# Causal attention in a two-layer kernel: the order of the key tiles within a head group, and the place of the one step without a dense part

## The chip, the core and the metric

The kernel is one program on one core of a Trainium2 chip. The metric is the device time of one launch in microseconds. Three runs of the kernel before took 1786.90, 1788.79 and 1789.57 us, so its median is 1788.79 us. One more execution was profiled; its own time and its span are in the table below.

## The reference, cut to what matters

Two layers work on x (2 batches of 1024 positions by 512 features). The first layer is a small recurrent block beside a gated feed-forward block; the change doesn't touch it. The second layer is causal attention beside a gated, 2:4-sparse feed-forward block. The change is in the attention:

```
qkv = x @ W_qkv.T + b_qkv ; q, k, v = split(qkv)         # 16 heads of 32 features
scores = einsum('bqhe,bkhe->bhqk', q, k) / sqrt(32)
scores = where(tril, scores, -inf)                        # a key counts for later queries only
out = einsum('bhqk,bkhe->bqhe', softmax(scores), v)
out = out.reshape(b, l, d) @ W_out.T + b_out
```

A softmax row is a sum over key tiles, so the tiles may be taken in any order.

## The kernel before, in words

Everything is in 32-bit floats. The attention stage runs from about 658 us to about 1198 us of the span. Ahead of it are the first layer, behind it the second feed-forward block. Within the stage the work is cut into eight **units** (batch bb, head group hg): four heads of one batch each.

**Two passes for each unit.** The first, `maxima` (L1179), computes scores for a query tile of 128 (qt 0 to 7) against a key chunk c of up to 512, and takes row maxima: TensorE writes two pairs of banks (L1188, tile m), VectorE adds the causal mask where the chunk holds the diagonal (L1195) and reduces (L1196). There are 12 of these a unit, of widths 128, 256, 384, 512, then (512, 128), (512, 256), (512, 384), (512, 512). The second pass has 12 **steps** a unit. A step is (j, kt): query half j (512 queries) against the key tile kt (128 keys). For j = 0 there are key tiles 0 to 3, for j = 1 key tiles 0 to 7. On the diagonal (kt >= 4j) only the queries from the tile on count, so the tile has 512, 384, 256 or 128 columns for kt - 4j = 0, 1, 2, 3; s in the code is the first column. Below, p is the place of a step in its unit, 0 to 11: p 0 to 3 are the first half, p 4 to 11 the second.

**One turn of the loop (L1492) for step n:**
1. `weights(n)` (L1238): TensorE writes the negated maxima (L1247) and adds the scores (L1253, tile s) into two bank pairs of two heads each. ScalarE takes the exponential of each pair into SBUF (L1264): into a tile `acc` for kt 0, else into one of five buffers `pt`. On the diagonal GpSimd cuts 128 columns to the causal triangle (L1273, affine select).
2. At fixed steps, parts of `shift_part` (L1216 on ScalarE, L1218 on GpSimd), which prepares the maxima of the next unit.
3. `gather(n-1)` (L1286): TensorE multiplies the weights of the step before with the values (L1297, tile o, one bank for a half), and the weights are added into `acc` (L1284) by GpSimd. The tile kt 6 of the second half goes to VectorE instead (`add_later`, L1301), after this turn's maxima. After the last key tile ScalarE copies o out (L1308).
4. At p 3 and p 7, transposes px of the shifted maxima (L1227) and `total` (L1312): TensorE sums `acc` (L1317, tile w), which gives the softmax denominators; four reciprocals on VectorE (L1329) and a product on GpSimd (L1333) follow over the next turns.
5. `do_first(n+13)`: the maxima, 13 places ahead. In p 0 to p 11 their widths are 256, 384, 512, 512, 128, 512, 256, 512, 384, 512, 512 and 128.
6. One **dense part** (L1047, 16 narrow matmuls): a seventh of a q/k projection of a later unit, half of a value tile, or half of a tile of the output projection. The first part of a projection also issues four weight sums on GpSimd (L1110 to L1112, L1153). `quiet` (L1484) names the turns without a dense part, p 6 of units 0 to 5; a part that is due is still forced by `late` (L1475).

**What sets the order.** `in_program_order` (L48) makes each engine execute the attention in the order in which the code issues it. The score pairs s, the maxima pairs m, px and w take turns in three wide PSUM tiles (`ps_wide`, L70), so each of them waits until the one three places before it has been read. `idle_vector` (L1234) tells the last 13 steps, which run beside no maxima: there VectorE takes over the masks and the sums. The values of key tile x are given due times (L1418 to L1427) such that they are there when o needs them.

Of the kernel before, what the change touches and what calls it, by code (L numbers as in the profile page):

```python
# [28 lines left out]
HG = NH * HD // P  # L29
# [6 lines left out]
def two_layers(ctx: ExitStack, tc: tile.TileContext, t: dict, out: bass.AP):  # L36
# [33 lines left out]
    def ps_wide(name):  # L70
        nonlocal wides
        wides += 1
        return ps_pair(name, wides % 3)

    def ps_bank(name, which):

        return ps.tile([P, 512], F32, tag=f"bank{which}", name=name)
# [278 lines left out]
    with tc.tile_pool(name="a", bufs=1) as a:  # L356
# [431 lines left out]
        for n in range(NU - 1):  # L788
            u = 2 * n + 2
# [89 lines left out]
        tt, next_tt, second = None, None, None  # L879
# [72 lines left out]
    with tc.tile_pool(name="b", bufs=1, reuse_waits="tile") as b:  # L952
# [74 lines left out]
        units = [(bb, hg) for bb in range(B) for hg in range(HG)]  # L1027
# [24 lines left out]
        def piece(name, lhs, rhs, done):  # L1052

            got = []

            def part(n):
                if n == 0:
                    got.append(next_bank(name))
                for k in (2 * n, 2 * n + 1):
                    dense(got[0], lhs(k), rhs(k), k == 0, k == KC - 1)  # L1060
                if n:
                    done(got[0])

            return [(part, 0), (part, 1)]
# [92 lines left out]
        def values(bb, n, j):  # L1157


            def done(pv):  # L1160
                if (bb, n, j) not in vals:
                    vals[bb, n, j] = b.tile(
                        [P, D], F32, tag="v", name=f"v_{bb}_{n}_{j}", bufs=12
                    )
                v = vals[bb, n, j]
                if alone is None:
                    nc.vector.tensor_add(v, pv, bv)
                else:
                    nc.scalar.copy(v, pv)
                    nc.gpsimd.tensor_add(v, v, bv)  # L1170

            return piece(
                f"pv_{bb}_{n}_{j}", lambda k: xt1[2 * bb + n][:, k, j * P : (j + 1) * P],
                lambda k: wv[:, k, :], done,
            )
# [55 lines left out]
            negs[u, half] = b.tile([P, TT], BF16, tag="neg", name=f"neg_{u}_{half}", bufs=4)  # L1231
            nc.vector.tensor_copy(negs[u, half], px[:, :NJ].rearrange("p t c -> p (t c)"))

        def idle_vector(u, j, kt):  # L1234

            return per * u + 4 * j + kt + ahead >= len(second)

        def weights(u, j, kt):  # L1238

            q, k, neg = qk[u, 0], qk[u, 1], negs[u, j]  # L1240
            name = f"{u}_{j}_{kt}"
            s = max(0, kt - 4 * j) * P
            cols = slice(j * 512 + s, (j + 1) * 512)
            pair = [ps_wide(f"s_{name}_{p}") for p in range(2)]
            for h in range(4):
                rows = slice(h * HD, h * HD + 3)
                nc.tensor.matmul(  # L1247
                    pair[h // 2][:, h % 2, s:], onesb[rows, :], neg[rows, s:],
                    start=True, stop=False,
                )  # L1250
            for h in range(4):
                rows = slice(h * HD, (h + 1) * HD)
                nc.tensor.matmul(  # L1253
                    pair[h // 2][:, h % 2, s:], k[rows, kt * P : (kt + 1) * P], q[rows, cols],
                    start=False, stop=True,
                )
            got = []
            for p in range(2):

                if kt == 0:  # L1260
                    pt = b.tile([P, 2, 512], F32, tag=f"acc{p}", name=f"acc_{name}_{p}", bufs=2)
                else:
                    pt = b.tile([P, 2, 512], F32, tag="pt", name=f"pt_{name}_{p}", bufs=5)
                nc.scalar.activation(  # L1264
                    pt[:, :, s:], pair[p][:, :, s:], AF.Exp, scale=1.0 / math.sqrt(HD)
                )
                d = pt[:, :, s : s + P]
                if kt >= 4 * j and idle_vector(u, j, kt - 1):
                    nc.vector.tensor_tensor(
                        d, d, allowed.unsqueeze(1).to_broadcast([P, 2, P]), ALU.min  # L1270
                    )
                elif kt >= 4 * j:
                    nc.gpsimd.affine_select(  # L1273
                        out=d, in_=d, compare_op=ALU.is_ge, fill=0.0,
                        base=0, pattern=[[0, 2], [1, P]], channel_multiplier=-1,
                    )
                got.append(pt)
            return u, j, kt, s, got
# [3 lines left out]
        def add_weights(eng, u, j, s, pts):  # L1282
            for acc, pt in zip(sums_of[u, j], pts):
                eng.tensor_add(acc[:, :, s:], acc[:, :, s:], pt[:, :, s:])  # L1284

        def gather(u, j, kt, s, pts):  # L1286

            bb, hg = units[u]
            if kt == 0:
                held[u, j] = ps_bank(f"o_{u}_{j}", 0)  # L1290
                sums_of[u, j] = pts
            po = held[u, j]
            last = kt == 4 * j + 3
            v = vals[bb, kt // NJ, kt % NJ][:, hg * P : (hg + 1) * P]
            for h in range(4):
                rows = slice(h * HD, (h + 1) * HD)
                nc.tensor.matmul(  # L1297
                    po[rows, s:], v[:, rows], pts[h // 2][:, h % 2, s:],
                    start=(kt == 0), stop=last, tile_position=(0, h * HD),
                )  # L1300
            if (j, kt) == (1, 6) and not idle_vector(u, j, kt):  # L1301

                add_later.append((nc.vector, u, j, s, pts))
            elif kt:
                add_weights(nc.vector if idle_vector(u, j, kt) else nc.gpsimd, u, j, s, pts)
            if last:
                att[u, j] = b.tile([P, 512], F32, tag="att", name=f"att_{u}_{j}", bufs=12)
                nc.scalar.copy(att[u, j], po)  # L1308
# [31 lines left out]
        def project_out(m):  # L1340
# [11 lines left out]
            (u, qt, c) for u in range(len(units)) for qt in range(QT) for c in range(qt // 4 + 1)  # L1352
        ]
        second = [
            (u, j, kt) for u in range(len(units)) for j in range(2) for kt in range(4 * j + 4)
        ]
        per, ahead = len(second) // len(units), 13

# [3 lines left out]
        rest, fixed, middle, after = [], {}, {}, {}  # L1362

        def put(n, *what):
            fixed.setdefault(n, []).append(what)
# [48 lines left out]
        rest = [(lo, hi, project(u)) for lo, hi, u in rest]  # L1414
# [1 line left out]
            put(per * 2 + n, next_sums)  # L1416
        put(per * 4 + 4, own_place)
        for x in range(4):  # L1418
            rest.append((-ahead, x, values(0, 0, x)))
            rest.append((-ahead, 7 + x, values(0, 1, x)))  # L1420
            for j in range(2):
                put(2 * x + j - 12, last_stats, 2 + x // 2, 2 * (x % 2) + j)
                put(2 * x - 9, last_row, 2 + x // 2, 2 * (x % 2) + j)
            put(2 * x - 10, last_norm, 2 + x // 2, x % 2)
            rest.append((per, per * 4 + x, values(1, 0, x)))

            rest.append((per * 3 + 5 + x, per * 4 + 2 + x, values(1, 1, x)))  # L1427
        put(per * 4 + 5, load_out)
# [52 lines left out]
            )  # L1481


        quiet = {per * u + 6 for u in range(6)}  # L1484
        behind = None
        start = mark()
        for _ in input_sums(0):
# [4 lines left out]
        for n in range(-ahead, len(second)):  # L1492
            if n == 0:
                alone = None
            now = weights(*second[n]) if n >= 0 else None
            for f, *args in middle.pop(n, ()):
                f(*args)
            if behind is not None:
                gather(*behind)
            behind = now  # L1500
            for f, *args in after.pop(n, ()):
                f(*args)
            if n < 0:
                one_part(n)
            if n + ahead < len(first):
                do_first(n + ahead)
            while add_later:
                add_weights(*add_later.pop())
            if (n >= 0 or n % 2) and n not in quiet:
                one_part(n)  # L1510
            while late(n) and one_part(n):
                pass
            what_is_fixed(n)
        in_program_order(start)
        gather(*behind)
        alone = 0
        narrow = False
# [14 lines left out]
    with tc.tile_pool(name="c", bufs=1, reuse_waits="tile") as c_:  # L1532
        units = [(pb, g, half) for pb in (1, 0) for g in range(G) for half in range(2)]
# [130 lines left out]
        for n in range(groups - 1):  # L1664

            end = n == groups - 2
            u = 2 * n + 2
# [49 lines left out]
        tt, next_tt, second = first_tt, None, None  # L1717
# [5 lines left out]
        for n, (pb, g, half) in enumerate(units):  # L1723
            i0 = 2 * pb
            x, y = xt1[i0], xt1[i0 + 1]
# [107 lines left out]
```

## Time and profile before

| | |
|---|---|
| median of three runs | 1788.79 us |
| the profiled execution: time | 1786.11 us |
| the profiled execution: span of its instructions | 1784.4 us |
| TensorE busy | 1753.4 us, 98% |
| VectorE, ScalarE, GpSimd busy | 1155.0, 481.0, 840.8 us |
| units 0 to 6 of the second pass, from the first L1247 matmul of each to the next one's | 58.0, 59.2, 59.6, 58.9, 59.2, 59.2, 58.6 us |
| unit 7 (no maxima), from 1136.5 us | 33.4 us to its last step's start |

Sum over the five middle units: 296.0 us. In the profile, PE is TensorE's matmuls, PEld its weight loads, DVE is VectorE, ACT is ScalarE, POOL is GpSimd and SP the queue of most DMAs. A row of the timeline gives the start, the duration, the engine, the source line, the operation, "out<-in" by tile names, and in brackets how long the engine sat idle before and what it waited for. Where rows are merged (x8), the duration is the union. Matmuls are pipelined, so the time that a group of them really costs is read from its start to the next group's start.

### The profile page before, as it was taken

What the parts mean: (1) busy time and instruction counts of PE and PEld (TensorE: products, weight loads), DVE (VectorE), ACT (ScalarE), POOL (GpSimd) and SP (SyncE); (2) the same over time, 40 slices, a digit from 0 to 9 for tenths busy, and PEclk for the clock granted to TensorE, in tenths of its full rate; (3) what the DMA queues carried; (4) which work ended last, traced back from release to release, by engine and by line L of the source; (5) the groups of instructions that cost most, each with busy time, mean ns of one, the idle gap of its engine ahead of it and who ended that gap; (6) DMA issues with size and microseconds to landing.
All of it is one profiled execution on the core that took longest, in us unless ns stands there. A gap on an engine that the chain in (4) does not pass through costs nothing.

```text
span 1784.4 us, 21717 instructions
## 1 busy us (share of the span) xinstructions
PE 1753.4 (98%) x8734; PEld 882.1 (49%) x8734; DVE 1155.0 (65%) x1516; ACT 481.0 (27%) x687; POOL 840.8 (47%) x736
## 2 busy tenths in 40 slices
PE   9999999999999999999999999999999999999999
PEld 5456566555555573322232222234565555555555
DVE  4875544556544367577677766842877778668676
ACT  3322222122221112433443443512221211211220
POOL 5145554355552243577868866613243344243400
PEclk9999999999999999999999999999999999999999
DMA  6120111011100000000000000011011102201101
GB/s 237 48 83 24 48 36 36 30 42 36 36 24 30 19 30 25 1 13 13 1 25 25 13 13 1 25 47 47 24 59 36 48 24 83 83 24 47 47 1 47
DMA packets 29619, 68.28 MB, mean 38 GB/s; under 512 B 3408, under 2 KB 11856, under 8 KB 27984
## 3 DMA queue, kind: packets, MB, share of 16 engines
q1 hardware_dynamic: 28800, 66.61, 10.8%
q8 instruction: 69, 1.13, 0.3%
q10 hardware_dynamic: 720, 0.30, 0.1%
q14 instruction: 30, 0.25, 0.0%
HBM read 62.70 MB, written 4.19 MB: 37 GB/s over the span
## 4 chain that ended last, share of the span: by engine, by line
PE 86%; POOL 7%; DVE 3%; issue 2%; ACT 1%; DMA 0%; SPq 0%; DVEq 0%; ACTq 0%
PE p_a L183 22%; PE p_c L183 22%; PE d L309 19%; POOL acc L1284 5%; PE m L1188 3%; PE pq_a L1047 2%; PE dr L1654 2%; PE pv L1047 2%; PE s L1253 2%; PE po L1047 2%; PE o L1297 2%; PE pq_c L1047 1%; POOL pt L1273 1%; DVE tops L1196 1%; PE s L1247 1%
## 5 line engine op out<-in xcount | busy, mean ns | idle before, releaser
L327 POOL TENSOR_TENSOR x<-x,de 128x512 f32<-128x512 f32 x87 | 126.5, 1469 | 297.8 <-DVE x L322 162.2
L1284 POOL TENSOR_TENSOR acc<-acc,pt 128x1024 f32<-128x1024 f32 (+3 forms) x124 | 217.1, 1775 | 0.0
L1196 DVE TENSOR_REDUCE tops<-m 128x2 f32<-128x1024 f32 (+2 forms) x192 | 180.9, 956 | 48.2 <-PE m L1188 43.6
L322 DVE TENSOR_TENSOR x<-x,d 128x512 f32<-128x512 f32 x145 | 99.3, 685 | 142.9 <-PE d L309 142.9
L1264 ACT ACTIVATE pt<-s 128x1024 f32<-128x1024 f32 (+3 forms) x160 | 116.1, 766 | 180.7 <-PE s L1253 128.4
L309 PE MATMUL d<-td,h 128*128 128x256 f32 x592 | 139.2, 379 | 0.0
L309 PEld LDWEIGHTS d<-td,h 128*128 128x128 f32 x592 | 112.5, 190 | 42.6 <-issue 28.7
L183 PE MATMUL p_a<-xt,s_a 128*128 128x512 f32 x256 | 116.6, 598 | 0.0
L183 PE MATMUL p_a<-xt,w 128*128 128x512 f32 x256 | 115.4, 593 | 0.7 <-ACT xt L136 0.7
L183 PE MATMUL p_c<-xt,gu 128*128 128x512 f32 x256 | 115.7, 592 | 0.0
L183 PE MATMUL p_a<-t_a,s_a 128*128 128x512 f32 x256 | 115.3, 594 | 0.0
L183 PE MATMUL p_c<-xt,s_c 128*128 128x512 f32 x256 | 115.1, 592 | 0.0
L1188 PE MATMUL m<-qk,qk 32*128 32x512 f32 (+3 forms) x768 | 102.5, 533 | 3.5 <-ACT acc L1264 3.1
L1195 DVE TENSOR_TENSOR m<-m,mask 128x256 f32<-128x256 f32 x128 | 54.6, 426 | 65.6 <-PE m L1188 59.8
L176 POOL TENSOR_TENSOR s_c<-gu,s_c 128x512 f32<-128x512 f32 x16 | 20.4, 1275 | 132.4 <-PE p_c L183 132.4
L1253 PE MATMUL s<-qk,qk 32*128 32x512 f32 (+3 forms) x768 | 81.7, 489 | 0.0
L1297 PE MATMUL o<-pt,v 128*32 128x512 f32 (+3 forms) x640 | 71.4, 482 | 9.8 <-POOL pt L1273 6.8
L1188 PEld LDWEIGHTS m<-qk,qk 32*128 32x128 f32 x768 | 40.4, 183 | 72.3 <-issue 27.5
L183 PEld LDWEIGHTS p_a<-xt,s_a 128*128 128x128 f32 x256 | 47.2, 190 | 57.8 <-issue 57.3
L183 PEld LDWEIGHTS p_c<-xt,s_c 128*128 128x128 f32 x256 | 48.6, 190 | 51.4 <-issue 49.9
L183 PEld LDWEIGHTS p_c<-xt,gu 128*128 128x128 f32 x256 | 48.7, 190 | 51.0 <-issue 49.5
L183 PEld LDWEIGHTS p_a<-xt,w 128*128 128x128 f32 x256 | 48.4, 190 | 50.0 <-issue 47.6
(287 smaller groups left out, 3196.7 us busy)
## 6 DMA issues: line engine op xcount, KB each, us to landing
w<-in_W SPq DMA_DIRECT2D x32, 512.0 KB, 3.2
gu<-in_gu SPq DMA_DIRECT2D x32, 512.0 KB, 3.2
wd<-in_down SPq DMA_DIRECT2D x8, 1024.0 KB, 4.8
x<-in_x SPq DMA_DIRECT2D x16, 256.0 KB, 4.3
w2h<-in_W2q SPq DMA_DIRECT2D x4, 1024.0 KB, 11.6
xr<-in_x SPq DMA_DIRECT2D x16, 256.0 KB, 2.6
wqk<-in_WqkvT SPq DMA_DIRECT2D x16, 256.0 KB, 3.1
out_x<-x SPq DMA_DIRECT2D x15, 256.0 KB, 2.0
```

Source lines behind the costliest of these rows:

```text
L183: nc.tensor.matmul(pair[:, m, :], a[:, m, k, :], x[:, k, :], start=start and k == 0, stop=stop and k == 1, skip_group_check=True,)
L309: nc.tensor.matmul(out_[:, j, :], lhs[:, q, j * P : (j + 1) * P], rhs[:, q], start=m in (0, 1, 3, 4) and j == q == 0, stop=j == q == 1, sk ...
L322: nc.vector.tensor_add(r, r, out_)
L327: nc.gpsimd.tensor_add(r, r, u2[half])
L1047: nc.tensor.matmul(bank[c, :], lhs[:, c], rhs, start=start, stop=stop, skip_group_check=True, tile_position=(0, h * w),)
L1188: nc.tensor.matmul(pair[h // 2][:, h % 2, :e], q[rows, qt * P : (qt + 1) * P], k[rows, c * 512 : c * 512 + e], start=True, stop=True,)
L1195: nc.vector.tensor_add(d, d, mask.unsqueeze(1).to_broadcast([P, 2, P]))
L1196: nc.vector.tensor_reduce(out=tops[u][:, c, qt, 2 * p : 2 * p + 2], in_=pair[p][:, :, :e], axis=mybir.AxisListType.X, op=ALU.max,)
L1253: nc.tensor.matmul(pair[h // 2][:, h % 2, s:], k[rows, kt * P : (kt + 1) * P], q[rows, cols], start=False, stop=True,)
L1264: nc.scalar.activation(pt[:, :, s:], pair[p][:, :, s:], AF.Exp, scale=1.0 / math.sqrt(HD))
L1284: eng.tensor_add(acc[:, :, s:], acc[:, :, s:], pt[:, :, s:])
L1297: nc.tensor.matmul(po[rows, s:], v[:, rows], pts[h // 2][:, h % 2, s:], start=(kt == 0), stop=last, tile_position=(0, h * HD),)
```

## The change

The key tiles of a half are no longer taken in rising order, except in the last unit: the first half takes 0, 3, 1, 2 and the second 0, 7, 1, 6, 2, 5, 3, 4. Tile 0 stays first, since it starts the sums and covers all columns. The functions that used kt as a place in time now use the place in this list; the value tiles' due times follow. The turn without a dense part moves from p 6 to p 4, beside the maxima of width 128.

```
+        def key_tiles(u, j):
+            if u == len(units) - 1:
+                return list(range(4 * j + 4))
+            return [0, 7, 1, 6, 2, 5, 3, 4] if j else [0, 3, 1, 2]
+
+        def idle_vector(u, j, kt, sooner=0):
-            return per * u + 4 * j + kt + ahead >= len(second)
+            return per * u + 4 * j + key_tiles(u, j).index(kt) - sooner + ahead >= len(second)
...
-                if kt >= 4 * j and idle_vector(u, j, kt - 1):
+                if kt >= 4 * j and idle_vector(u, j, kt, 1):
...
-            last = kt == 4 * j + 3
+            last = kt == key_tiles(u, j)[-1]
...
-            (u, j, kt) for u in range(len(units)) for j in range(2) for kt in range(4 * j + 4)
+            (u, j, kt) for u in range(len(units)) for j in range(2) for kt in key_tiles(u, j)
...
-            rest.append((-ahead, x, values(0, 0, x)))
-            rest.append((-ahead, 7 + x, values(0, 1, x)))
+            rest.append((-ahead, key_tiles(0, 0).index(x), values(0, 0, x)))
+            rest.append((-ahead, 3 + key_tiles(0, 1).index(4 + x), values(0, 1, x)))
...
-            rest.append((per, per * 4 + x, values(1, 0, x)))
+            rest.append((per, per * 4 + key_tiles(HG, 0).index(x), values(1, 0, x)))
...
-        quiet = {per * u + 6 for u in range(6)}
+        quiet = {per * u + 4 for u in range(6)}
```

The same matmuls, exponentials, masks, sums and DMAs are issued as before, in the same numbers; the DMA queue of SP has the same transfers in the same order. The last step of the second half is now tile 4 with 512 columns, that of the first half tile 2 with 256 (before: tiles 7 and 3 with 128), and the sum that VectorE takes for kt 6 comes at p 8 in place of p 11.

## The prediction

> **What bounds the kernel now.** First the page: TensorE is busy almost all of the span, so a gain must come from TensorE time that isn't work.
>
> ```profile
> span 1784.4 us, 21717 instructions
> PE 1753.4 (98%) x8734; PEld 882.1 (49%) x8734; DVE 1155.0 (65%) x1516; ACT 481.0 (27%) x687; POOL 840.8 (47%) x736
> ```
>
> The 98% hides waits, because matmul ends are modelled. So next I read TensorE's timeline in unit 3, from start to start. Here are p 4, 6 and the beginning of p 7:
>
> ```profile
> 920.42 0.40 PE L1247 MATMUL s<-neg,onesb 3*128 3x512 bf16 x4
> 920.64 1.03 PE L1253 MATMUL s<-qk,qk 32*128 32x512 f32 x8
> 921.60 0.43 PE L1297 MATMUL o<-pt,v 128*32 128x128 f32 x8
> 921.96 0.49 PE L1188 MATMUL m<-qk,qk 32*128 32x128 f32 x4
> 922.79 0.49 PE L1188 MATMUL m<-qk,qk 32*128 32x128 f32 x4 [0.34 <-ACT acc L1264]
> 923.21 1.92 PE L1047 MATMUL pq_c<-t_b,sq 128*32 128x512 f32 x16
> ...
> 930.44 0.40 PE L1247 MATMUL s<-neg,onesb 3*128 3x512 bf16 x4
> ...
> 933.79 0.39 PE L1247 MATMUL s<-neg,onesb 3*128 3x512 bf16 x2 [0.21 <-ACT pt L1264]
> 934.64 0.39 PE L1247 MATMUL s<-neg,onesb 3*128 3x512 bf16 x2 [0.46 <-DVE tops L1196]
> 934.64 1.24 PE L1253 MATMUL s<-qk,qk 32*128 32x512 f32 x8
> ```
>
> The second half of m starts 2.15 after s (922.79 - 920.64): its PSUM pair is the one that the first exponential reads. The quiet p 6 lasts 3.35, but p 7 then waits 0.85 - 0.23 for the reduction of p 6's maxima. The third view is GpSimd's timeline at the end of the unit, where it runs without a gap:
>
> ```profile
> 950.02 4.69 POOL L1284 TENSOR_TENSOR acc<-acc,pt 128x1024 f32<-128x1024 f32 x2
> 954.67 1.28 POOL L1333 TENSOR_TENSOR att<-att,inv 128x512 f32<-128x512 f32 x1
> 955.89 0.77 POOL L1273 TENSOR_SCALAR_AFFINE_SELECT pt<-pt 128x256 f32<-128x256 f32 x2
> 956.62 3.61 POOL L1284 TENSOR_TENSOR acc<-acc,pt 128x768 f32<-128x768 f32 x2
> ```
>
> A mask that o needs stands behind whole sums there. So two clocks count: TensorE's with ScalarE, and GpSimd's queue.
>
> **Part 1: step lengths on TensorE.** From unit 3's rows: neg takes 0.23, 0.17, 0.12, 0.07 for 512, 384, 256, 128 columns; s 0.96, 0.75, 0.54, 0.38; o 1.00, 0.78, 0.54, 0.36. The second half of m starts no earlier than a gap g after s: 2.15, 1.78, 1.4 by the first three widths of s, and 0.97 for 128 (exponential at 0.49, two waits of some 0.05, 0.38 long). From there to the dense part c = 1.06, 0.89, 0.62, 0.42 by the width of m. The dense part takes 1.86. A step is neg + max(s + o, g) + c + 1.86. This gives 4.66 for p 4 (measured 4.65), 4.70 for p 1 (4.68), 4.86 for p 0 (4.86). Where a step of before has the same s and m widths bound by g, I take its measured length. After, with the widths of s / o (o is the step before's):
>
> | p | before | after: s / o / m | after, us |
> |---|---|---|---|
> | 0 | 4.86 | 512/512/256 | 4.86 |
> | 1 | 4.68 | 128/512/384 | 4.20 = 0.07+0.38+1.00+0.89+1.86 |
> | 2 | 4.39 | 384/128/512 | 4.87 = 0.17+1.78+1.06+1.86 |
> | 3 | 5.78 | 256/384/512 | 5.57: with px 0.22, w 0.98, m 1.07 |
> | 4 | 4.65 | 512/256/128, quiet | 3.35, as p 6 of before |
> | 5 | 5.37 | 128/512/512 | 4.43 |
> | 6 | 3.35 | 512/128/256, dense | 4.86, as p 0 |
> | 7 | 7.12 | 256/512/512 | 5.87: px 0.28, w 1.00 |
> | 8 | 5.16 | 512/256/384 | 5.16 |
> | 9 | 4.87 | 384/512/512 | 4.87 |
> | 10 | 4.41 | 512/384/512 | 5.37, as p 5 of before |
> | 11 | 4.22 | 512/512/128 | 4.65, as p 4 of before |
> | sum | 58.86 | | 58.06 |
>
> p 5 holds 0.06 for o's bank, which ScalarE copies late in the short p 4. In p 3 the wait for the reduction (0.58 before px) goes: o is 0.24 longer, and the reductions of p 2 start earlier against the dense part. In p 5 the pair wait (0.62) doesn't return: the maxima of p 4 are 128 wide, a mask and a reduction of 0.42 each, done before p 4's second exponential frees the other pair. So p 4 to 7 gain 2.0, p 0 to 3 gain 0.2, and **p 8 to 11 lose 1.4**: the wide tiles that follow now bind them by their exponentials. What is late next is GpSimd. Over units 1 to 5, 296.0 become 5 x 58.06 = 290.3, or -5.7. Unit 0 gives -0.9 likewise (58.0 to 57.1), unit 6, which has no quiet p 4, -0.4. Together **-7.0**.
>
> The dense part of p 4 and p 5 goes one step later. It issues no DMA; its evacuation by ScalarE or VectorE (0.69) follows. VectorE's sum for kt 6 moves from p 11 to p 8, behind p 8's masks and reductions: it ends some 6.3 into p 8, the reductions of p 9 follow at their normal place (slack 0.6 at p 10), so it costs nothing; if that slack goes, p 10 waits.
>
> **Part 2: GpSimd's queue.** Count from p 7 of the changed order; p 9, 10, 11, 0', 1', 2' start at 11.0, 15.9, 21.3, 25.9, 30.8, 35.0. Rows: a pair of masks 0.77, sums 4.66, 3.6, 1.42 for 512, 384, 128 columns, product 1.25. Masks of kt 5 end 14.1 (exponentials of p 9), sums of kt 2 end 18.7, the product 20.0, sums of kt 5 23.6, masks of kt 4 24.9 (exponentials of p 11), sums of kt 3 29.6, masks of kt 0 30.3, sums of kt 4 35.2, masks of kt 3 36.0. TensorE's o of kt 0 wants its masks at 31.2: slack 0.9. The o of kt 3 may wait until 36.6 under p 2's own g: slack 0.6. So where nothing else is queued it just holds. But:
> - At the ends of units 0, 2, 4 a projection begins at p 11, and its four weight sums (4 x 0.73 = 2.9; they stand ahead of the masks of the next tile 0) come first. Masks of kt 0 then end 33.2, the second half of o starts at 33.25 and the step ends 2.0 late; masks of kt 3 end 38.8 and cost 0.3 more. **3 x 2.3 = 6.9.**
> - In unit 2 two sums of the inputs (2.37 each, L1075 and L1076) are issued at p 0 and p 1. The first makes the masks of kt 3 end at 38.3: p 2 is **1.8** late.
> - At the start of unit 7 VectorE must sum kt 4 (2.55) instead of kt 7 (0.78). It waits there for GpSimd's sums of kt 3 and holds back the masks of the next tile behind it on VectorE, which o waits for: step 3 of unit 7 starts 12.1 to 12.5 after p 11 of unit 6, where it was 10.8. With 0.4 of it in unit 6's count already, **+1.3**.
>
> GpSimd's gain: VectorE's kt 6 sums slowed its masks at the unit's end in before (1.68 for a pair, at 960.17); that falls where the queue has slack, nothing.
>
> **Sum:** -7.0 + 6.9 + 1.8 + 1.3 = +3.0. The profiled execution took 1786.11, so 1789.1; the median of the runs lies 2.68 above it, so I say **1791.8 us**. No change that can be told: a measurement of this kernel separates about 0.2%, or 3.6 us.
>
> **An unknown price.** The new waits leave TensorE idle for some 1.7 us at p 1 of units 1, 3 and 5, and 2.1 at p 2 of unit 2. Idle stretches of 0.87 left the clock alone; one of 2.23 in unit 7 did not, the granted clock fell to 0.78 and 0.73 of full speed in the two stretches from it:
>
> ```profile
> 1162.13 2.51 PE L1297 MATMUL o<-pt,v 128*32 128x512 f32 x8 [2.23 <-DVE pt L1269]
> 1163.84 3.03 PE L1047 MATMUL po<-wout,att 128*32 128x512 f32 x16
> ...
> 1160.00:1163.80 3.80, 1.67 (x8) 0.74 (x12) 3.80 (x6) 1.47 (x2) 0.51 (x1) 0.78 0.00 0
> 1163.80:1167.00 3.20, 3.20 (x28) 1.16 (x24) 3.20 (x5) 0.81 (x1) 0.00 (x0) 0.73 0.02 5
> ```
>
> Start to start, o took 1.71 there for 1.00, and the dense part 2.96 for 1.86: 1.8 for one such spell. So each new wait costs 0 to 1.8 more, together 0 to 7.2. All four lie between the rows, nearer 2.23 than 0.87; but that one came in unit 7, whose steps had waits of their own just before (0.33 and 0.19 at its p 5 and p 7), and these come after busy steps. So I take 0 and keep the upper end.
> The Trainium skill (TensorE: Matmul & The Clock Gate, section "HAM oscillation — how this bites in real kernels") warns only of idle gaps above some 3.4 us; by that rule the four waits cost no clock and the sum stays +3.0, by the row of unit 7 it could be +10.2. The trace differs from the rule, as 2.23 was enough once.
>
> **The rivals.**
> - *The clock falls* (slower). Place: the four waits of part 2. Price 1.8 each. It decides from the second on: +3.0 + 3.6 = +6.6, and at most 1799.0. For it: the row above. Against: two dozen idle stretches of 0.46 to 0.87 without it.
> - *The short p 4 hands its wait on* (slower). VectorE has the reductions of p 3 (2.36) and two reciprocals (1.75) ahead of p 4's maxima. If they end some 0.7 later than I count, p 5 waits as p 7 did (0.62 + 0.21) and GpSimd's slack of 0.6 goes too: 6 x 0.8 = 4.8, so 1796.6. For it: p 7 of before. Against: the 128 columns.
> - *GpSimd isn't late* (faster). If its queue runs 2 us ahead of my count, part 2's first two terms go: -7.0 + 1.3 = -5.7, so 1783.1. For it: it is 74% busy in unit 3 (43.8 of 58.9). Against: every duration above is a row, and the masks stand behind the sums by program order.
> - *The order does nothing by itself*, only the quiet step counts: the evener widths would then give neither the 1.4 loss at p 8 to 11 nor the late masks. That is -2.0 a unit, 6 x 2.0 = 12 less, 1776.8. Against: g is seen at p 4 and p 5 of every unit.
>
> **How the numbers follow.** Forecast 0.52, with a spread of 2 us of its own (1789 to 1796; 0.36 of it within 0.2%, 0.16 above); the clock 0.20; the short p 4 0.12; GpSimd not late 0.12; the quiet step alone 0.04. So faster 0.16, same 0.36, slower 0.48. The range leaves out the faster cases and the topmost part of the two slower ones: 1786 to 1801.
>
> **What would show it.** Right: p 4 of 3.3 to 3.5 and p 7 near 5.9; p 10 near 5.4; at p 1 of units 1, 3, 5 o waits for GpSimd's mask of acc, in units 2, 4, 6 not; GpSimd without a gap from p 9 to p 2. Wrong: p 1 equally long in all units; p 5's second neg waiting for VectorE; clock rows below 1.00 before 1130 us; sums of 512 columns shorter than 2.33 each.

## The result, and the profile after

The changed kernel takes 1792.3 us (median of 20 runs, 1790.18 to 1794.43), the kernel before on the same chip 1788.84 us (20 runs). The ratio is 1.0023, with a 95% interval of 1.0016 to 1.0029: slightly slower, by what a measurement of this kernel can just tell. The forecast was 1791.8 us.

First the page of the kernel after, the span and the first row of the engines:

```profile
span 1790.5 us, 21721 instructions
PE 1760.4 (98%) x8734; PEld 885.2 (49%) x8734; DVE 1155.8 (65%) x1516; ACT 480.4 (27%) x687; POOL 833.6 (47%) x736
```

As in the page of before, nothing can be told from it. The span is 6.1 us longer, but of these 3.2 lie ahead of the attention: the second pass of unit 0 starts at 727.07 us of the span, in before at 723.87. The code there is the same; this profiled execution has a spell of low granted clock at 20 to 40 us (mean 0.83) that the other hasn't. Such a spell falls in some executions of a kernel and not in others (the two profiles of one kernel, e8 below, have mean clocks of 0.91 and 0.83 there). So I compare the attention from its own start. From here on, "attention" is the time from the start of unit 0 to the start of the last step of unit 7: 446.1 us before, 448.3 after.

| unit | 0 | 1 | 2 | 3 | 4 | 5 | 6 | 7 | sum |
|---|---|---|---|---|---|---|---|---|---|
| before | 58.0 | 59.2 | 59.6 | 58.9 | 59.2 | 59.2 | 58.6 | 33.4 | 446.1 |
| after | 58.05 | 60.46 | 59.90 | 60.46 | 57.81 | 60.46 | 57.61 | 33.53 | 448.3 |

Units 4 and 6 became faster, 1, 3 and 5 slower. Next the timeline of TensorE in unit 3 of after, p 4, p 5 and the start of p 6 (line numbers from here on are six higher than before's: neg L1253, s L1259, mask L1279 or on VectorE L1275, sums L1290, o L1303):

```profile
927.46 0.40 PE L1253 MATMUL s<-neg,onesb 3*128 3x512 bf16 x4
927.69 1.03 PE L1259 MATMUL s<-qk,qk 32*128 32x512 f32 x8
928.65 0.64 PE L1303 MATMUL o<-pt,v 128*32 128x256 f32 x8
929.22 1.11 PE L1188 MATMUL m<-qk,qk 32*128 32x128 f32 x8
930.75 0.24 PE L1253 MATMUL s<-neg,onesb 3*128 3x128 bf16 x4 [0.42 <-ACT acc L1270]
930.80 0.47 PE L1259 MATMUL s<-qk,qk 32*128 32x128 f32 x8
931.34 1.06 PE L1303 MATMUL o<-acc,v 128*32 128x512 f32 x8
932.33 1.14 PE L1188 MATMUL m<-qk,qk 32*128 32x512 f32 x8
933.40 1.92 PE L1047 MATMUL pq_c<-t_b,sq 128*32 128x512 f32 x16
935.26 0.39 PE L1253 MATMUL s<-neg,onesb 3*128 3x512 bf16 x4
```

The quiet step p 4 lasts 930.75 - 927.46 = 3.29, and the next step waits for an exponential (ACT), not for the maxima. p 5 lasts 4.51, and the 0.85 that p 7 of before waited is gone: p 7 lasts 5.66, in before 7.12 in unit 4. Now GpSimd at the end of unit 2, the place that answers to the third view of before:

```profile
904.51 4.68 POOL L1290 TENSOR_TENSOR acc<-acc,pt 128x1024 f32<-128x1024 f32 x2
909.15 0.74 POOL L1110 TENSOR_TENSOR sq<-wqk 128x256 f32<-128x256 f32 x1
909.96 0.73 POOL L1111 TENSOR_TENSOR sq<-sq,wqk 128x256 f32<-128x256 f32 x1
910.65 0.73 POOL L1112 TENSOR_TENSOR wqk<-wqk 128x256 f32<-128x256 f32 x1
911.33 0.73 POOL L1153 TENSOR_TENSOR wqk<-wqk,sq 128x256 f32<-128x256 f32 x1
912.01 0.77 POOL L1279 TENSOR_SCALAR_AFFINE_SELECT acc<-acc 128x256 f32<-128x256 f32 x2
912.93 4.69 POOL L1290 TENSOR_TENSOR acc<-acc,pt 128x1024 f32<-128x1024 f32 x2
```

The masks of `acc` end at 912.78, and TensorE has been ready for them since the end of s at p 1 of unit 3. Its own timeline there:

```profile
910.41 0.45 PE L1259 MATMUL s<-qk,qk 32*128 32x128 f32 x8
912.47 1.41 PE L1303 MATMUL o<-acc,v 128*32 128x512 f32 x8 [1.61 <-POOL acc L1279]
...
918.03 0.77 PE L1303 MATMUL o<-pt,v 128*32 128x128 f32 x8 [0.52 <-POOL pt L1279]
```

In unit 4, at whose start no weight sums are queued, the table of waits holds one row:

```profile
PE s L1253 <- ACT acc L1270: 0.4, 1, 0.4
```

So the picture of the forecast is there: steps of 57.81 where GpSimd keeps up, and 2.65 more where four weight sums (2.9) stand ahead of the masks. The last stretch to look at is the clock in unit 7 (columns as in the prediction, the granted clock third from the end), around the same wait of 2.23 that lowered it in before:

```profile
1163.40:1166.80 3.40, 3.27 (x32) 0.98 (x29) 3.40 (x4) 2.22 (x3) 1.31 (x1) 1.00 0.00 0
1166.80:1170.00 3.20, 1.10 (x10) 0.46 (x14) 3.20 (x5) 1.44 (x2) 0.51 (x1) 1.00 0.00 0
```

Here it stayed at 1.00.

### The profile page after: what moved, and what is told of

It reads as the page before. It is cut to its first block, busy times and chain, and to the rows that moved or that the text cites. A ratio compares the mean times of both kernels' runs of the same rounds, so it can differ in the third digit from the quotient of the medians.

```text
span 1790.5 us, 21721 instructions
## 1 busy us (share of the span) xinstructions
PE 1760.4 (98%) x8734; PEld 885.2 (49%) x8734; DVE 1155.8 (65%) x1516; ACT 480.4 (27%) x687; POOL 833.6 (47%) x736
## 4 chain that ended last, share of the span: by engine, by line
PE 91%; POOL 4%; DVE 3%; ACT 2%; issue 1%; POOLq 0%; ACTq 0%
PE p_a L183 22%; PE p_c L183 21%; PE d L309 19%; PE m L1188 5%; PE po L1047 3%; PE pv L1047 3%; PE o L1303 3%; POOL acc L1290 3%; PE s L1259 2%; PE pq_a L1047 2%; PE dr L1660 2%; PE pq_c L1047 2%; PE s L1253 1%; DVE acc L1290 1%; PE pp L607 1%; ACT acc L1270 1%
## 5 line engine op out<-in xcount | busy, mean ns | idle before, releaser
L1290 POOL TENSOR_TENSOR acc<-acc,pt 128x1024 f32<-128x1024 f32 (+3 forms) x124 | 214.2, 1750 | 0.0
L1188 PE MATMUL m<-qk,qk 32*128 32x512 f32 (+3 forms) x768 | 111.7, 533 | 2.5 <-ACT pt L1270 0.8
L1259 PE MATMUL s<-qk,qk 32*128 32x512 f32 (+3 forms) x768 | 80.4, 487 | 0.0
L1279 POOL TENSOR_SCALAR_AFFINE_SELECT pt<-pt 128x256 f32<-128x256 f32 x98 | 39.3, 409 | 80.4 <-ACT pt L1270 79.4
L1303 PE MATMUL o<-pt,v 128*32 128x512 f32 (+3 forms) x640 | 68.3, 477 | 7.9 <-DVE pt L1275 4.4
```

The source lines that it names most:

```text
L1188: nc.tensor.matmul(pair[h // 2][:, h % 2, :e], q[rows, qt * P : (qt + 1) * P], k[rows, c * 512 : c * 512 + e], start=True, stop=True,)
L1259: nc.tensor.matmul(pair[h // 2][:, h % 2, s:], k[rows, kt * P : (kt + 1) * P], q[rows, cols], start=False, stop=True,)
L1303: nc.tensor.matmul(po[rows, s:], v[:, rows], pts[h // 2][:, h % 2, s:], start=(kt == 0), stop=last, tile_position=(0, h * HD),)
```

## The experiments

**Theory:** the order makes the steps shorter (some 1 us a unit), moving the quiet step would bring most of this gain in the old order too, and what turns the gain into a loss is GpSimd's queue, which the wide tiles at the end of the second half fill up to the masks of the next unit. **Rivals:** the waits cost clock (it fell in before after 2.23 us of idleness); or the order is bad by itself, by its exponential-bound steps p 8 to p 11, and GpSimd only shows it. Runs e1 to e4 take the change apart, e5 to e8 work on GpSimd's queue, e9, e11 and e12 ask whether relief there helps any order. "Attention" is from the profile, the medians and ratios from the timed runs against the kernel before on the same chip.

| run | units 1, 3, 5 | unit 2 | unit 4 | unit 7 | attention | median | ratio [95%] |
|---|---|---|---|---|---|---|---|
| before | 59.2, 58.9, 59.2 | 59.6 | 59.2 | 33.4 | 446.1 | 1788.84 | 1 |
| after | 60.5 each | 59.9 | 57.8 | 33.5 | 448.3 | 1792.3 | 1.0023 [1.0016, 1.0029] |
| e1 | 62.3, 60.3, 60.3 | 60.0 | 57.7 | 36.4 | 452.5 | 1792.14 | 1.0013 [1.0004, 1.0022] |
| e2 | 58.7, 59.0, 58.9 | 59.1 | 58.4 | 33.5 | 443.3 | 1784.89 | 0.9975 [0.9966, 0.9984] |
| e3 | 58.7 each | 58.5 | 58.0 | 33.6 | 442.6 | 1783.82 | 0.997 [0.9958, 0.9981] |
| e4 | 60.9, 62.5, 60.9 | 60.3 | 58.2 | 36.4 | 454.8 | 1796.81 | 1.0048 [1.0033, 1.0064] |
| e5 | 57.8 each | 59.2 | 57.8 | 33.4 | 439.7 | 1779.82 | 0.9947 [0.9933, 0.9961] |
| e6 | 60.4 each | 57.8 | 57.8 | 33.5 | 446.1 | 1789.14 | 1.0008 [1.0, 1.0017] |
| e7 | 63.9, 63.0, 62.8 | 59.9 | 57.8 | 35.2 | 458.4 | 1800.53 | 1.0069 [1.0056, 1.0081] |
| e8 | 57.8 each | 57.8 | 57.8 | 31.9 | 436.8 | 1779.19 | 0.9956 [0.9943, 0.9968] |
| e9 | 59.8, 60.4, 60.4 | 58.5 | 58.0 | 34.3 | 447.7 | 1790.31 | 1.0012 [1.0003, 1.0021] |
| e11 | 63.0, 58.5, 58.5 | 58.8 | 58.3 | 33.6 | 447.3 | 1790.46 | 1.0003 [0.9994, 1.0012] |
| e12 | 59.2 each | 57.8 | 57.8 | 34.6 | 443.5 | 1785.19 | 0.998 [0.9971, 0.9988] |

### e1: the new order alone

```
-        quiet = {per * u + 4 for u in range(6)}
+        quiet = {per * u + 6 for u in range(6)}
```

> The changed kernel with the quiet step back at p 6: the new key order alone. Theory (step sums): p 4 becomes 4.65, p 6 some 3.4 and p 7 about 6.0 to 6.2, so p 4 to 7 add up to 18.5 against 18.4 of the changed kernel; 1792 to 1795 us. Rival (the place of the quiet step brings the 2.0 a unit at p 4 to 7): about 1804 us.

1792.14 us, against 1792.3 with the quiet step at p 4. Step by step in unit 4, p 4 to p 7 take 4.65, 4.37, 3.35 and 5.87 (18.24), after's 3.29, 4.51, 4.92 and 5.66 (18.38). Under the new order the place of the quiet step is worth nothing that can be told. The 62.3 of unit 1 is a clock spell in p 7 (mean granted clock 0.54 for 3.5 us); no long idleness stands ahead of it (0.28 at most in the three gaps before it), so its cause stays open. The 36.4 of unit 7 holds two more spells, one behind a wait of 1.79 at its p 1 and one behind the wait of 2.23 at p 9.

### e2: the quiet step alone

This is the kernel before with the last line of the change alone, the quiet step at p 4.

> The kernel before with the quiet step at p 4: its move alone. Theory: p 4 3.3, p 5 5.4, p 6 4.9, p 7 6.2 without its wait for the maxima, 19.8 in place of 20.5; GpSimd's masks at p 11 take some of it back; -2 to -4 us, 1785 to 1787. Rival (the quiet step alone brings the 2.0 a unit): 1777.

1784.89 us. In unit 4, p 4 to p 7 take 3.29, 5.36, 4.92 and 6.39 (19.96), before's 4.65, 5.37, 3.35 and 7.12 (20.49). It saves 0.8 of the unit: 59.18 to 58.37 (the other 0.3 is p 0, 4.86 for 5.18). So half of the change gives 0.25% by itself, and the other half takes it away and more.

### e3 and e4: each half's order alone, both with the quiet step at p 4

```
-            return [0, 7, 1, 6, 2, 5, 3, 4] if j else [0, 3, 1, 2]
+            return list(range(8)) if j else [0, 3, 1, 2]                  # e3
+            return [0, 7, 1, 6, 2, 5, 3, 4] if j else list(range(4))      # e4
```

> The changed kernel with rising key tiles in the second half: new order in the first half only, quiet step at p 4. Theory: p 0 to 3 gain 0.4, the quiet step 0.6 a unit, no late masks at the start of units 1, 3, 5, since the sums ahead of them are of 128 columns again; 1782 to 1785 us. Rival (alternating widths cost by themselves, in either half): 1788 or more.

> The changed kernel with rising key tiles 0, 1, 2, 3 in the first half: the new order in the second half only, quiet step at p 4. Theory (the late masks come from the second half's order): p 1 of units 1, 3 and 5 ends as late as in the changed kernel (about 6.2 long), p 3 of the other units 5.8 in place of 5.45; 1791 to 1795 us. Rival (the first half's narrow tile at p 1 makes the wait): p 1 of units 1, 3, 5 about 4.7, 1786 or less.

e3 takes 1783.82 us, e4 1796.81, more than expected. In unit 4, where nothing is late, the two halves are worth little: 58.37 in e2, 58.01 with the first half's order, 58.18 with the second's, 57.81 with both. In units 1, 3 and 5 they part: 58.7 with the second half rising, 60.9 with it alternating. So the loss comes with the second half, at whose end GpSimd sums the tiles 2, 5, 3 and 4 (512, 384, 512 and 512 columns) in place of 4, 5 and 7 (512, 384, 128; kt 6 is VectorE's). The excess of e4 over the expected 1795 is clock in part: its unit 3 has a step p 5 of 6.15 for 4.51 (granted clock 0.54 from 932.3 on), and unit 7 two more spells, behind waits of 1.79 and 2.23.

### e5: another tile's sum to VectorE

```
-            if (j, kt) == (1, 6) and not idle_vector(u, j, kt):
+            if (j, kt) == (1, 3) and not idle_vector(u, j, kt):
```

GpSimd takes back the sum of kt 6 at p 8, where after's trace has it idle for 5.76 (ahead of 952.97), and gives away one of the full sums at p 11.

> The changed kernel with the sum of kt 3 (512 columns, p 11) on VectorE in place of that of kt 6 (256 columns, p 8). GpSimd then does kt 6 in its idle stretch of 5.8 at p 8 and has 4.7 less ahead of the next unit's masks. Theory (GpSimd's queue makes the masks late): p 1 of units 1, 3 and 5 falls from 6.18 to 4.15, 1781 to 1785 us. Rival (the loss is that of the wide tiles at p 8 to 11 alone, or VectorE becomes late): no gain, 1791 to 1795.

1779.82 us, better than the range expected and faster than the kernel before by 0.5%. Units 1, 3 and 5 lose all of their 2.65: p 1 takes 4.15. GpSimd's timeline at the end of unit 2 (p 1 of unit 3 starts at 903.79):

```profile
897.96 0.73 POOL L1110 TENSOR_TENSOR sq<-wqk 128x256 f32<-128x256 f32 x1
898.76 1.59 POOL L1111 TENSOR_TENSOR sq<-sq,wqk 128x256 f32<-128x256 f32 x1
900.32 1.71 POOL L1112 TENSOR_TENSOR wqk<-wqk 128x256 f32<-128x256 f32 x1
901.99 0.73 POOL L1153 TENSOR_TENSOR wqk<-wqk,sq 128x256 f32<-128x256 f32 x1
902.68 0.76 POOL L1279 TENSOR_SCALAR_AFFINE_SELECT acc<-acc 128x256 f32<-128x256 f32 x2
```

The masks end 0.35 ahead of p 1, in after 2.4 behind its start, although two of the weight sums took 1.6 to 1.7 for 0.73: VectorE adds kt 3 at that time, from 898.52 on. Nothing of the order, of the exponentials or of TensorE's work was changed, so the rival that the order is bad by itself falls for units 1, 3 and 5.

### e6: the sums of unit 2's inputs ahead of unit 2

```
-        for n in (0, 1, 4, 5):
-            put(per * 2 + n, next_sums)
+        for n in (per + 8, per + 8, per * 2 + 4, per * 2 + 5):
+            put(n, next_sums)
```

> The changed kernel with the first two sums of the inputs for batch 1 (L1075, L1076 on GpSimd) issued at the end of p 8 of unit 1, in GpSimd's idle stretch, in place of p 0 and p 1 of unit 2. Theory: p 2 of unit 2 falls from 6.60 to about 4.9 and p 3 from 5.8 to 5.45; 2 us less than the changed kernel, 1789.5 to 1791. Rival (the wait in unit 2 comes from elsewhere): no difference.

Unit 2 falls from 59.90 to 57.80 and no other moves by more than 0.05; its table of waits holds the same one row as unit 4 of after. The time is 1789.14 us. The term of unit 2 is thereby shown, and measured at 2.1.

### e7: two of the weight sums twice

```
+                for _ in range(2 if u in (3, 5, 7) else 1):
-                nc.gpsimd.tensor_add(got[1], w21, w22)
-                nc.gpsimd.tensor_sub(got[2], got[1], w11)
+                    nc.gpsimd.tensor_add(got[1], w21, w22)
+                    nc.gpsimd.tensor_sub(got[2], got[1], w11)
```

The same values are written a second time, so only GpSimd's queue gets longer, by 2 x 0.73.

> The changed kernel with the first two weight sums of a projection (L1110, L1111) executed twice for units 3, 5 and 7, which begin at p 11 of units 0, 2 and 4. Theory: the masks of the next tile 0 come 1.46 later, p 1 of units 1, 3 and 5 goes from 6.18 to 7.6 and the other units stay; 4.4 us more than the changed kernel, 1796 to 1798, and if the idle time of 3.1 lowers the clock up to 1.8 more for each. Rival (GpSimd has slack there): 1792 to 1793.

1800.53 us. TensorE's waits from 727 to 1165 us (line numbers one higher here, and in e11 and e12) begin with

```profile
PE o L1304 <- POOL acc L1280: 9.6, 3, 3.2
```

three waits of 3.2, after's 1.61 and the 1.46 added, and a little. And the clock now does fall, after each of the three. The granted clock in the stretch with the wait and in the two behind it, at p 1 of unit 1, and in the same pair of unit 3:

```profile
786.00:789.30 3.30, 1.59 (x24) 0.46 (x16) 1.93 (x4) 0.70 (x3) 3.06 (x5) 1.00 0.00 0
789.30:792.70 3.40, 1.90 (x8) 0.38 (x8) 0.00 (x0) 0.27 (x1) 3.40 (x6) 0.55 0.02 5
792.70:796.10 3.40, 3.40 (x20) 0.92 (x20) 1.36 (x3) 0.00 (x0) 3.40 (x3) 0.50 0.00 0
912.20:915.60 3.40, 0.99 (x8) 0.29 (x8) 0.00 (x0) 0.27 (x1) 3.40 (x7) 1.00 0.00 0
915.60:919.00 3.40, 3.40 (x20) 0.91 (x20) 1.31 (x3) 0.00 (x0) 3.40 (x2) 0.55 0.03 5
```

p 1 takes 9.36 in unit 3 for 6.18: half of the 3.2 is the longer wait, the other half the clock. From the start of o to the start of p 2 it is 5.65 for 4.06 (in units 1 and 5 6.55 and 5.47), so a spell costs 1.4 to 2.5 here. So the rival of the clock has a real mechanism and about the price that I gave it; the waits of 1.6 and 2.0 in after's profile did not set it off, these of 3.2 did each time.

### e8: e5 and e6 together

> The changed kernel with both remedies: the sum of kt 3 on VectorE in place of that of kt 6, and the two input sums at p 8 of unit 1. Theory: unit 2 goes from 59.2 to about 57.9, 1.3 less than with the first remedy alone; 1777.5 to 1779.5 us, faster than both kernels. Rival (GpSimd's idle stretch at p 8 is too short for both, and p 9 to p 11 of unit 1 become late): 1780 to 1782.

Every unit from 1 to 5 takes 57.8, no o of these units waits for GpSimd, and the time is 1779.19 us; in a second set of runs on another chip it is 1778.42 (ratio 0.9957 [0.9945, 0.997]).

> The kernel with both remedies once more, on the same chip as the one beside it: 1778 to 1780 us by either theory; it gives the distance to the rising order.

Like e5, it beats both kernels. It isn't told apart from e5 by its time, though its attention is 2.9 shorter in the profile: of these 1.4 are unit 2's, and 1.5 unit 7's, where the clock spell of e5's profile did not occur in e8's.

### e9: does the relief help the rising order as well?

The order of e3 with e5's edit.

> The changed kernel with rising key tiles in the second half, and the sum of kt 3 on VectorE (at p 8) in place of that of kt 6 (at p 11): no alternation in the second half, but GpSimd relieved. Theory (alternating brings nothing to TensorE's steps there, what counts is when GpSimd is loaded): p 11 falls from 4.25 of the third experiment to 3.3 to 3.9 and p 1 of units 1 and 3 from 4.46 to 4.15; 1777 to 1780 us, the same as with the alternating order and the same relief. Rival (the alternating order itself makes the relieved kernel fast): 1783 or more.

1790.31 us. My theory missed here: the relieved kernel is slower than the unrelieved e3. GpSimd from p 8 of unit 2 to p 1 of unit 3 (which starts at 909.00) shows why, and below it o at that p 1:

```profile
892.65 1.66 POOL L1279 TENSOR_SCALAR_AFFINE_SELECT pt<-pt 128x256 f32<-128x256 f32 x2 [3.34 <-ACT pt L1270]
...
905.15 2.51 POOL L1290 TENSOR_TENSOR acc<-acc,pt 128x512 f32<-128x512 f32 x2
...
910.49 0.77 POOL L1279 TENSOR_SCALAR_AFFINE_SELECT acc<-acc 128x256 f32<-128x256 f32 x2
```

```profile
910.95 1.41 PE L1303 MATMUL o<-acc,v 128*32 128x512 f32 x8 [1.43 <-POOL acc L1279]
```

In the rising order kt 3 is summed at p 8, where GpSimd then idles for 3.34, and the sum of kt 6 comes back to it at the unit's end, where it and the four weight sums stand ahead of the masks of `acc` that the next p 1 needs: o waits 1.43 for them. So it was no relief at the place that counts. It also made VectorE late: p 9 of units 0, 1, 3 and 5 takes 5.52 for e3's 4.87, as the dense part waits 0.58 for VectorE, which has the sum of kt 3 in front. The same edit helps or hurts by where the order puts the two tiles.

### e11 and e12: the relief at the end of the unit, in both orders

```
+                eng = nc.vector if u in (3, 5, 7) else nc.gpsimd
-                nc.gpsimd.tensor_add(got[1], w21, w22)
-                nc.gpsimd.tensor_sub(got[2], got[1], w11)
-                nc.gpsimd.tensor_sub(w21, w11, w21)
+                eng.tensor_add(got[1], w21, w22)
+                eng.tensor_sub(got[2], got[1], w11)
+                eng.tensor_sub(w21, w11, w21)
```

e11 is e3 with this and e6's edit, e12 the changed kernel with both.

> The order of run e3 (only the first half alternates, the second half rises, quiet step p 4), with GpSimd relieved in another way than in run e9: the first three weight sums of the projections of units 3, 5 and 7 (L1110 to L1112) go to VectorE, and the sums of unit 2's inputs come ahead of unit 2. Run e9 took GpSimd work away at p 8, where its queue had 3.33 of idle time, and gave it the sum of kt 6 back at p 11, where it was late; this run takes 2.2 away at p 11 itself. Theory: what counts is GpSimd's work between p 9 and the next p 2, and the rising second half costs only 0.2 per unit against the alternating one. Then units 1, 3 and 5 take 58.0 (58.65 in e3), unit 2 also 58.0 (58.5), o at p 1 waits under 0.2 for GpSimd, and the time is 1780 to 1783. Rival, that the alternating order of the second half is itself worth 3 us or more: 58.4 or more per unit and 1784 or more.

> The same relief in the changed order (both halves alternating, quiet p 4): the first three weight sums of the projections of units 3, 5 and 7 go to VectorE, the sums of unit 2's inputs come ahead of unit 2, and kt 6 stays VectorE's. Theory: units 1, 2, 3 and 5 fall to 57.8 as in run e8, unit 7 keeps its 33.5, since its sums stay as in the changed kernel: 1789.1 (run e6) less 3 x 2.6 = 1781.3, so 1780 to 1783, within 2 of the rising order of the run beside it. Rival, that it was the kt 3 sum on VectorE that mattered and not the lateness of GpSimd: p 1 of units 1, 3 and 5 stays above 5.5 and the time at 1787 or more.

Both miss my numbers. e12 takes 1785.19 us: the waits for GpSimd are gone from units 1, 3 and 5, but p 1 still takes 5.55. VectorE's timeline at the end of unit 2, and TensorE's at p 1:

```profile
898.72 2.08 DVE L1111 TENSOR_TENSOR sq<-wqk 128x256 f32<-128x256 f32 x1
900.83 2.48 DVE L1112 TENSOR_TENSOR sq<-sq,wqk 128x256 f32<-128x256 f32 x1
903.23 0.41 DVE L1113 TENSOR_TENSOR wqk<-wqk 128x256 f32<-128x256 f32 x1
```

```profile
905.39 0.23 PE L1254 MATMUL s<-neg,onesb 3*128 3x128 bf16 x2 [1.17 <-DVE tops L1197]
```

Sums of 0.41 take 2.08 and 2.48 while GpSimd adds (two sums, 4.87 from 898.15 on), the maxima behind them are late, and s waits for these. The wait changed its engine and kept half its size: 59.2 instead of 57.8. So the rival is right that p 1 stays above 5.5, though for another reason than the one it names, and both its time (1787 or more) and mine (1780 to 1783) are wrong.

In e11 units 3 and 5 take 58.5, e3's 58.65 and my 58.0: no o at their p 0 and p 1 waits for GpSimd, but s at p 1 waits 0.32 for VectorE's maxima instead. And the early sums of the inputs hit unit 1: in the rising order GpSimd has masks to cut in p 8 to p 11, and two sums of 2.4 stand ahead of them.

```profile
838.57 1.79 PE L1304 MATMUL o<-pt,v 128*32 128x384 f32 x8 [2.85 <-POOL pt L1280]
```

Start to start, that o took 1.72 for 0.78, so the clock fell as well, and p 10 of unit 1 takes 9.21 for 4.41. In e6 and e8, where p 8 and p 10 hold tiles off the diagonal, the same edit was free. Without those 4.8, e11's attention would be 442.5, e3's 442.6: its units gained nothing that can be told. The rival's 58.4 or more per unit came out, but the reason that it gives is not shown by this, since VectorE's wait and the 4.8 come from where the sums were put. Whether a rising second half with a well placed relief would reach e8 stays open; the two orders differ by 0.2 in a unit where nothing waits for GpSimd (58.01 and 57.81).

## Why the prediction was right, point by point

The time came out right (+3.5 between the medians, forecast +3.0), and the terms behind it can be checked in the attention, which grew by 2.2. Forecast and measured, they are: steps of units 1 to 5 -5.7 and -7.0, unit 0 -0.9 and 0, unit 6 -0.4 and -1.0, late masks +6.9 and +8.0, unit 2's sums +1.8 and +2.1, unit 7 +1.3 and +0.1. So the two large terms are right in mechanism and near in size, but that the total is as near as it is was luck: errors of 0.3 to 1.3 in every term cancelled to -0.8, and 0.8 behind the attention, which I hadn't counted, made up for that.

- **Step lengths.** Right. Unit 4: p 4 to p 7 18.38 (forecast 18.5), p 8 to p 11 20.10 (20.05), p 10 at 5.34 (5.37). Over units 1 to 5 the steps alone give 5 x 57.81 = 289.0 for 296.1, -7.0, where I had -5.7: a unit is 0.25 shorter than counted. Most of this is at p 7 (5.66 for 5.87) and p 3 (5.45 for 5.57); p 5 and p 11 came out 0.08 and 0.09 longer than counted.
- **Unit 0.** Wrong: forecast -0.9, measured 0. Its p 1 takes 4.68 where the other units take 4.15, as o waits 0.46 for VectorE's copy of a value tile out of its bank, and p 2 takes 5.15 for 4.87 in unit 4; against before, its p 2 and p 3 became 0.5 and 0.2 longer. I had carried unit 3's steps over without looking for what unit 0 alone has. Unit 6 made up for it: -1.0 for -0.4.
- **Masks late at the ends of units 0, 2 and 4.** Right, and shown by taking it away (e5) and by making it worse (e7). The size was 2.65 for 2.3, 8.0 in three units for 6.9: p 3 was 0.36 late too (5.80 for 5.45), since the transposes px wait there for maxima that came late.
- **Unit 2's input sums.** Right: 2.1 for 1.8, shown by e6.
- **Unit 7.** The size was near, the mechanism not the one I wrote. Forecast +1.3, of which the sum of kt 4 on VectorE was to be the cause. Measured +0.1, with 1.4 given back at p 9 (8.05 to 6.67), where the clock of after's profile didn't fall; so +1.5 of its own. But what is late are the masks of `acc`. VectorE's timeline of after, and GpSimd's beside it:

```profile
1144.17 3.00 DVE L1275 TENSOR_TENSOR acc<-acc,allowed 128x256 f32<-128x256 f32 x2 [1.53 <-ACT acc L1270]
```

```profile
1141.86 4.67 POOL L1290 TENSOR_TENSOR acc<-acc,pt 128x1024 f32<-128x1024 f32 x2
```

Two masks that took 0.75 in before take 3.00: the second one ends after GpSimd's sums do, and o waits 1.78 for them. In before only two short operations of 0.23 and 0.47 ran on GpSimd around them. In e8, where the sum of kt 3 is VectorE's in unit 6 and GpSimd has no sum to do there, the two masks take 0.42 and 0.43 and p 1 of unit 7 takes 2.66 for after's 4.22. The Trainium skill (SBUF — State Buffer, section "Who interferes with whom") states that a VectorE instruction with two inputs in SBUF contends with a GpSimd instruction that reads SBUF, and that the order of issue decides which of the two blocks. This row agrees, as do the 2.08 and 2.48 of e12.

- **The clock.** The forecast took 0 for the four new waits; right: none of them lowered it in the profile of after, while 3.2 did in three cases of three (e7). The row on which I had built the upper end is no rule by itself: the wait of 2.23 at p 9 of unit 7 stands in all 14 profiles of these kernels, and the clock fell behind it in 10. These are all of TensorE's waits of more than 1 us from unit 0 to the last step of unit 7, in the 14 profiles:

| TensorE's wait, us | cases | clock fell behind it |
|---|---|---|
| 1.1 to 1.4 | 18 | 0 |
| 1.6 to 2.0 | 22 | 3 |
| 2.23 | 14 | 10 |
| 2.85 (e11) | 1 | 1 |
| 3.2 (e7) | 3 | 3 |

The four waits of after belong to the second row, and the three falls there are all in unit 7 (two at p 1, one at p 11 in the second profile of e8, at 1166.6 us); of 13 such waits in units 1 to 5 none lowered the clock. So the longer the wait, the more often the clock fell, and taking 0 fits waits of this length and place. The price of 1.8 was too high for the row that I read it from: p 9 of unit 7 takes 8.05 with the spell and 6.67 without, so 1.4. The Trainium skill's rule of idle gaps above some 3.4 us (TensorE: Matmul & The Clock Gate, section "HAM oscillation — how this bites in real kernels") would have let all of these pass; here the clock fell behind 17 of the 58.

- **The other rivals.** The short p 4 hands no wait on that costs anything: 0.42 at p 5, for the exponential. GpSimd was late as counted. "The order does nothing by itself" is wrong as put, since the p 8 to p 11 loss is there; but e2 shows that the quiet step alone would have been the better change.

Behind the start of the last step, after's profile is 0.8 longer than before's, and this belongs to the same clock spell. The last wait of o there, in after:

```profile
1178.04 0.41 PE L1303 MATMUL o<-pt,v 128*32 128x128 f32 x4 [1.61 <-DVE pt L1275]
```

In before it is 0.84. VectorE sets the end of unit 7, so a TensorE that was slow at p 9 waits less for it here: in the ten profiles whose clock fell at p 9 it is 0.84, in the other four (after, e6 and both of e8) 1.61. A spell at that place costs 1.4 less 0.8. With the 0.8, the attention and what follows it grew by 3.0 in the profile, the forecast's sum.

## What to carry to other kernels

Making the steps on the busiest engine more even is worth what the even steps save, less what the new order puts ahead of the next thing that this engine needs in the queue of an engine that has slack only on the average; count that queue instruction by instruction over the stretch where it is fullest. Split a change with two parts: here one part alone gave 0.25%, and the sum lost 0.23%. And work moved off a late engine helps only if it is moved out of the stretch in which the engine is late (e9), and to an engine that isn't slowed there itself by running beside the late one (e12).

## What the runs showed that I had not expected

- VectorE's additions and masks and GpSimd's additions were slowed by large factors where both ran at once on inputs in SBUF: 128x256 sums on VectorE of 2.08 and 2.48 for 0.41 (e12), on GpSimd 1.59 and 1.71 for 0.73 (e5), masks on VectorE 3.00 for 0.75 (after).
- The granted clock fell to about half for 3.4 to 6.8 us after one idle stretch of 3.2 (in some executions of 1.6 to 2.2, by the table above). Twice in the 14 profiles it fell with no idle stretch above 0.5 just ahead of it: in e1 at 817.4 us and in e4 at 932.3 us, in the step behind a quiet one. Its row in e1:

```profile
817.40:820.90 3.50, 3.50 (x36) 0.87 (x28) 0.62 (x2) 1.08 (x2) 2.80 (x4) 0.54 0.00 0
```

What decides there isn't settled: the same steps in the other units of these two kernels kept their clock.
